# Two small loads moved behind the weights' loads, and one preparation moved ahead of the sums, in a four-stage transformer kernel

## The chip, the cores and the metric

The kernel runs on one core of one Trainium2 chip. Its time is the device time of one execution in microseconds (us). Before the change it was 930.57 us, the median of three runs (930.12 to 933.92). A core has a matrix engine (TensorE, PE in the profile), a vector engine (VectorE, DVE), an activation engine (ScalarE, ACT), a general engine (GpSimd, POOL) and a queue engine (SyncE, SP), which here issues nearly all loads and stores (the gathers and some of the last stores are GpSimd's). Each runs its own list of instructions in order, and semaphores between them say when data is ready.

## The reference

Four layers follow each other, each with a residual where there is one to add and a layer norm around it. Cut to what matters here:

```python
# x: (8, 512, 256)
qkv = x @ W_qkv                              # layer 0, retention with 16 heads of 16
ret = einsum('bhtd,bhsd->bhts', q, k) * decay
r   = einsum('bhts,bhsd->bhtd', ret, v) + einsum('bhtd,hde->bhte', q, past_kv) * 256
y   = groupnorm(r) * gn_weight[head] + gn_bias[head]
x   = layernorm(x + y)

def absmean(W):                              # layer 0, FFN with ternary weights
    gamma = mean(abs(W)) + 1e-6
    return sign(W / gamma) * minimum(round(abs(W / gamma)), 1)
h = layernorm(gelu(x @ absmean(W_fc).T)) * ln_w + ln_b
x = layernorm(x + h @ absmean(W_proj).T)     # W_fc (1024, 256), W_proj (256, 1024)

x = layernorm(x + linear_attention(x))       # layer 1, attention over heads per token
x = layernorm(x + mixture_of_experts(x))     # layer 1, 8 experts, top 2, capacity 160
```

A ternary weight needs the mean of the absolute values of the whole matrix before its first element can be made: the matrix must be loaded and summed, the sum spread over the 128 partitions, and only then can the elements be compared with half the mean.

## The kernel before

The work goes batch by batch (8 batches of 512 tokens, held as 4 chunks of 128 tokens). Each batch passes through the stages a1 (projection to q, k, v and retention), a2 (group norm, residual), b (FFN), bn, c1, c2 (layer 1's attention), and then the experts. Two preparations run once: `prepare_ffn` makes the ternary weights, and `prepare_l1` transposes layer 1's.

**The order of instructions is written by a planner.** The stages are generators; `interleave` picks the next one for TensorE by planned times. Work for the other engines is handed to `op(engine, cost, t, fn, ...)`, where t is the time from which it may start (its due time) and cost is the planner's duration. `op` looks for the first gap of the engine's planned time that is long enough, from t on, and the operations are issued in the order of the times so found. DVS means VectorE with a port that it shares with GpSimd: in the plan such operations, and GpSimd's, exclude each other. Loads (`dma`) take no time in the plan; those with one due time are issued in the order of the calls. The plan only sets the order of each engine's list. On the chip, an instruction starts when its engine is free and its semaphores are set.

**The start of the kernel.** SP issues, in this order: the identity matrix `ident`, x of batch 0, `wqkv`, the table of constants `cst`, `past` (the past state, 16 KB), the two vectors of the group norm into `gn` (weight and bias, 16 values each, given to all 128 partitions), W_fc in four pieces of 256 KB (tile `prepare`), W_proj in four pieces (tile `pr_w`), the two vectors `lnwb` of the FFN's layer norm, x of batch 1, and layer 1's small vectors.

VectorE's list at the start: three sums of W_fc (`threshold`, "fc_t"), `prepare_past`, the fourth sum, two kT operations (they scale the keys of batch 0 out of PSUM), `halves` (the threshold itself), 8 operations of `ternary` for W_fc, four sums of W_proj ("pr_t"), three masks of the first scores (scm), `halves` and 8 ternary operations for W_proj, masks and states, the prT products, and `prepare_gn`. `prepare_past` (L612, L617) writes `past_bd`, the past state as block-diagonal matrices, which TensorE reads from about 33 us on (L990). `prepare_gn` (L623, L624) writes `gnp`, read by the group norm of batch 0 at 64.9 us.

TensorE's list at the start: transposes of x (L348), 16 matmuls for q and k (L905), the sums of W_fc over the partitions (fc_ps, L650), v (L929), the first scores (L955), four matmuls that only fill a wait (L294), the sums of W_proj (pr_ps, L650), the transposes of the ternary W_fc (L713), further scores and retention (L990, L1003, L1012), and the transposes of the ternary W_proj (L726). GpSimd masks one of every four score tiles (scm) and makes padded queries (qz). ScalarE moves results out of PSUM. Line L205 is the planner's common line for all operations handed to `op` directly.

Of the kernel before, what the change touches and what calls it, by code (L numbers as in the profile page):

```python
# [20 lines left out]
P = 128  # L21
# [60 lines left out]
def tile_layers(ctx: ExitStack, tc: tile.TileContext, ins, out, at):  # L82
# [52 lines left out]
    ACT, DVE, POOL, SP, GELU, EXP, DVS, POOLD = range(8)  # L135
# [12 lines left out]
    class Plan:  # L148
        now = 0.0
        slow = 0.0  # L150
        t = 0.0
# [14 lines left out]
    def give(tag, t, n=1):  # L166
        Plan.free[tag] += [t] * n

    def take(tag, n=1):

        times = sorted(Plan.free[tag])
        assert len(times) >= n, tag
        Plan.free[tag] = times[n:]
        return times[n - 1]

    def op(engine, cost, t, fn, *args, use=None, drop=None, bank=None, **kw):


        if engine in (GELU, EXP):
            cost += 0.0 if engine == Plan.loaded else TABLE  # L180
            engine, Plan.loaded = ACT, engine
        users = [engine]
        if engine in (DVS, POOL):
            users.append("port")
        engine = users[0] = {DVS: DVE, POOLD: POOL}.get(engine, engine)
        t = t + HOP
        if use is not None:
            t = max(t, take(use) + HOP)
        if engine != SP:
            length = max(cost - OVERLAP[engine], 0.05)  # L190
            found = False
            while not found:
                found = True
                for user in users:
                    for a, b in Plan.busy[user]:
                        if t + length <= a:
                            break
                        if b > t:
                            t, found = b, False
            for user in users:  # L200
                bisect.insort(Plan.busy[user], (t, t + length))
                while Plan.busy[user][0][1] < Plan.t - 30.0:
                    Plan.busy[user].pop(0)
        Plan.count += 1
        heapq.heappush(Plan.events, (t, Plan.count, lambda: fn(*args, **kw)))  # L205
        t += cost
        if drop is not None:
            give(drop, t)
        if bank is not None:
            release(bank, t)  # L210
        return t
# [5 lines left out]
    def pe(cost):  # L217


        start = max(Plan.now, Plan.t)  # L220
        if start - Plan.now > 1.5:
            Plan.slow = start + (1.5 if start - Plan.now < 3.0 else 8.0)
        cost += min(max(Plan.slow - start, 0.0) / 2, cost)
        Plan.now = Plan.t = start + cost
        return Plan.now + PE_OUT

    def bank(name):
        i = Plan.banks.index(min(Plan.banks))
        assert Plan.banks[i] < HELD, name
        ps = psum.tile([P, 512], F32, tag=f"bank{i}", bufs=1, name=name)  # L230
        Plan.bank_of[id(ps)] = ps, i
        Plan.banks[i] = HELD
        return ps

    def release(ps, t):
        Plan.banks[Plan.bank_of.pop(id(ps))[1]] = t

    def need(t, n=1):

        while True:  # L240
            r = max(t + HOP_PE, sorted(Plan.banks)[n - 1] + HOP if n else 0.0)
            yield "pe", r if r < HELD else Plan.t + 0.5
            if not n or sorted(Plan.banks)[n - 1] <= Plan.t + 1e-6:
                return
# [324 lines left out]
    with ExitStack() as stages:  # L569
# [15 lines left out]
        def dma(t, out, in_):  # L585
            op(SP, 0.0, t, nc.sync.dma_start, out=out, in_=in_)
# [8 lines left out]
        past = ab.tile([P, 2, HD], F32, name="past")  # L595
        dma(0.0, past, ins["L0_attn_past_kv"].rearrange("(m h) d e -> (h d) m e", m=2))
        gn = ab.tile([P, 2, H], F32, name="gn")
        dma(0.0, gn[:, 0, :], ins["L0_attn_gn_weight"].partition_broadcast(P))
        dma(0.0, gn[:, 1, :], ins["L0_attn_gn_bias"].partition_broadcast(P))

        past_bd = ab.tile([P, 2, P], F32, name="past_bd")

# [20 lines left out]
                nc.vector.tensor_tensor(gnt, bc(gn[:, j, :], 1, 2), headsel, ALU.mult)  # L623
                nc.vector.tensor_reduce(gnp[:, j, :], gnt, AX.X, ALU.add)  # L624

        op(DVS, 1.0, 15.5, prepare_past)
        op(DVS, 0.85, 40.0, prepare_gn)


# [9 lines left out]
        def threshold(name, parts, ts):  # L639

            tot = fb.tile([P, len(parts)], F32, name=f"{name}_t")
            for i, (part, t) in enumerate(zip(parts, ts)):
                t = op(
                    DVE, 0.61, t, V.tensor_reduce, tot[:, i : i + 1], part, AX.X, ALU.add,
                    apply_absolute_value=True,
                )
            yield from need(t)
            ps = bank(f"{name}_ps")
            for i in range(len(parts)):
                T.matmul(  # L650
                    ps[:, 0:1], ones, tot[:, i : i + 1], start=(i == 0), stop=(i == len(parts) - 1)
                )
            half = fb.tile([P, 2], F32, name=f"{name}_h")

            def halves():
                nc.vector.tensor_scalar(
                    half[:, 1:2], ps[:, 0:1], 1.0 / (FF * D), 1e-6, ALU.mult, ALU.add
                )
                nc.vector.tensor_scalar(half[:, 0:1], half[:, 1:2], 0.5, None, ALU.mult)
                nc.vector.tensor_scalar(half[:, 1:2], half[:, 1:2], -0.5, None, ALU.mult)  # L660

            return half, op(DVE, 0.5, pe(0.5), halves, bank=ps)

        def ternary(qs, ws, half, t):

            ends = []
            for q, w in zip(qs, ws):
                e = op(DVS, 0.36, t, V.tensor_scalar, q, w, half[:, 1:2], None, ALU.is_lt)
                ends.append(op(
                    DVS, 0.64, e, V.scalar_tensor_tensor, q, w, half[:, 0:1], q, ALU.is_gt,  # L670
                    ALU.subtract,
                ))
            return ends

        def prepare_ffn():
# [12 lines left out]
            def half_row(x, i):  # L688
                return x[:, i // 2, i % 2 * 512 : (i % 2 + 1) * 512]
# [9 lines left out]
                        )  # L699

            op(SP, 0.0, 0.0, vectors)
            parts = [[big[:, k, i * 512 : (i + 1) * 512] for i in fours] for k in range(2)]
            half, t = yield from threshold("fc", parts[0], [12.0, 13.5, 14.7, 16.0])
            ready = ternary(parts[1], parts[0], half, t)
            parts = [[half_row(w, i) for i in fours] for w in (w_pr, q_pr)]
            half, t = yield from threshold("pr", parts[0], [17.0, 18.0, 19.0, 20.0])
            ready_pr = max(ternary(parts[1], parts[0], half, t))
            for n4 in range(NF // 4):
                for k in range(NK):
# [11 lines left out]
            for n2 in range(NF // 2):  # L721
                yield from need(ready_pr)
                ps = bank("pr_tp")
                for n in range(2):
# [5 lines left out]
                t = op(  # L730
                    ACT, 0.6, pe(0.46), A.copy,
                    raw[:, n2 * 2 : n2 * 2 + 2, :].rearrange("p n d -> p (n d)"), ps, bank=ps,
                )
# [17 lines left out]
            for f in range(NF):  # L751
                T.matmul(acc[:, :D], ones, prT[:, f, :D], start=(f == 0), stop=(f == NF - 1))
            mean = wk.tile([P, D], F32, tag="ex", bufs=EX, name="pr_mean_s")
            t = op(
                ACT, 0.4, pe(3.5), A.activation, mean, acc[:, :D], AF.Copy, scale=1.0 / FF,
                use="ex", bank=acc,
            )
# [5 lines left out]
            t = e  # L763
# [989 lines left out]
        def after(*keys):  # L1753
# [3 lines left out]
        half = B // G  # L1757
# [10 lines left out]
            ],  # L1768
            [
                (("p", 0), [], {"b8": 2}, prepare_ffn()),  # L1770
                (("p", 1), [], {"m4": 1}, prepare_l1()),
            ],
# [89 lines left out]
```

## Time and profile before

| | before |
|---|---|
| runs, median (lowest to highest) | 930.57 us (930.12 to 933.92) |
| the profiled execution's own time | 931.42 us |
| its span in the profile | 929.6 us |
| mean granted TensorE clock | 0.982 |
| bytes moved by DMA | 60.69 MB |

The span goes from the first to the last instruction; 1.8 us of the profiled execution lie around it. In the profile a line such as `15.92 0.45 DVE L612 ... past_bd<-cst,past` says when an instruction began, how long it took, its engine and line, and which tile it writes from which. Instructions of one kind that follow each other are put together (x3), and the first start and the stretch from the first start to the last end are given. In brackets stands how long the engine had been idle, and what ended the wait. A table of stretches gives, for each, the busy time of the engines, the granted clock of TensorE as a share of full speed, and the mean busy share of the 16 DMA engines. The DMA queue's waits say what SP waited for before it could issue.

### The profile page before, as it was taken

The page shows a single profiled execution, that of the slowest core. Times are in us where ns is not written, and L with a number is a line of the kernel's source. Part 1 is how long each engine was busy: PE and PEld are TensorE (multiplying, and loading weights), DVE is VectorE, ACT ScalarE, POOL GpSimd, SP SyncE. Part 2 cuts the span into 40 slices and gives each one's busy share as a digit, 9 for nine tenths or more (in the row PEclk, how much of TensorE's full clock was granted, in tenths as well). Part 3 has the DMA queues.
Part 4 walks back from the last instruction along what each step waited for, and adds up shares of the span by engine and source line. Part 5 has one row for each costly group of instructions (what it writes and reads, how often), then busy time and mean ns, then how long its engine had stood idle before and what let it go on. Part 6 is the DMA issues. An engine that isn't in the chain of part 4 may idle for free. (4 is left out here: it accounts for less than half of the span.)

```text
span 929.6 us, 18769 instructions
## 1 busy us (share of the span) xinstructions
PE 881.7 (95%) x7628; PEld 687.9 (74%) x7628; DVE 607.9 (65%) x1530; ACT 453.0 (49%) x866; POOL 397.2 (43%) x404
## 2 busy tenths in 40 slices
PE   7899999999999999999999999999999999999892
PEld 4777777777767677677767676786787889999781
DVE  3945367669777847877887778578678654621223
ACT  2327356537652684486287535838536343122223
POOL 2425542744453263445434542732653332362233
PEclk9999999999999999999999999999999999999795
DMA  7030000001000100010020001050143356168742
GB/s 212 12 114 1 1 2 1 2 24 46 2 1 24 47 2 2 23 47 1 1 69 2 1 2 46 2 182 1 46 126 115 108 185 196 24 191 290 241 116 105
DMA packets 49894, 60.69 MB, mean 65 GB/s; under 512 B 5680, under 2 KB 44784, under 8 KB 49808
## 3 DMA queue, kind: packets, MB, share of 16 engines
q1 hardware_dynamic: 45952, 53.92, 17.4%
q0 software_dynamic: 3856, 5.57, 3.1%
q8 instruction: 60, 0.98, 0.4%
q14 instruction: 26, 0.21, 0.1%
HBM read 43.76 MB, written 15.73 MB: 64 GB/s over the span
## 5 line engine op out<-in xcount | busy, mean ns | idle before, releaser
L1167 PE MATMUL pr_ps<-prT,fT 128*128 128x257 f32 x512 | 117.4, 381 | 0.2 <-DVE f_ss L205 0.2
L1167 PEld LDWEIGHTS pr_ps<-prT,fT 128*128 128x128 f32 x512 | 95.2, 190 | 14.7 <-DVE f_ss L205 0.5
L205 POOL TENSOR_TENSOR fsq<-fsq,fsf 128x512 f32<-128x512 f32 x56 | 72.2, 1288 | 37.5 <-ACT fsf L205 35.3
L1530 PE MATMUL wi_ps<-xsT,wi 128*128 128x160 f32 x512 | 78.2, 308 | 0.1
L1559 PE MATMUL wo_ps<-e_hT,wo 128*128 128x160 f32 x512 | 74.5, 301 | 0.0
L1530 PEld LDWEIGHTS wi_ps<-xsT,wi 128*128 128x128 f32 x512 | 73.3, 196 | 1.3 <-ACT xsT L205 0.6
L205 DVE TENSOR_TENSOR hm<-hs,cst 128x512 f32<-128x512 f32 x96 | 60.2, 675 | 19.6 <-PE hs L1306 19.1
L1559 PEld LDWEIGHTS wo_ps<-e_hT,wo 128*128 128x128 f32 x512 | 70.8, 190 | 1.8 <-issue 1.5
L205 DVE TENSOR_TENSOR scm<-sc,cst 128x512 f32<-128x512 f32 x96 | 60.8, 679 | 15.4 <-PE sc L955 15.4
L205 ACT ACTIVATE e_hT<-wi_ps 128x480 f32<-128x480 f32 (+1 forms) x48 | 25.3, 526 | 87.4 <-PE wi_ps L1530 87.4
L205 POOL TENSOR_TENSOR ln_rs<-ln_rs,mhalf 128x4 f32<-128x4 f32 x32 | 33.3, 1040 | 80.7 <-DVE ln_rs L205 80.7
L205 POOL DMA_INDIRECT y_d<-eo,srci x21 | 32.8, 1561 | 71.4 <-ACT eo L205 35.7
L205 POOL TENSOR_TENSOR scm<-scm,cst 128x512 f32<-128x512 f32 x32 | 41.2, 1289 | 49.7 <-ACT scm L205 49.7
L205 DVE STREAM_TRANSPOSE hT<-pad 128x512 f32<-128x512 f32 x64 | 59.3, 959 | 3.5 <-ACT pad L205 3.0
L905 PE MATMUL qk_ps<-xT,wqkv 128*128 128x512 f32 x128 | 60.6, 617 | 1.0 <-ACT xT L205 1.0
L1247 PE MATMUL qk_ps<-l1T,x2T 128*128 128x512 f32 x128 | 61.5, 603 | 0.0
L205 POOL TENSOR_TENSOR hm<-hm,cst 128x512 f32<-128x512 f32 x32 | 41.1, 1284 | 33.5 <-ACT hm L205 33.5
L1138 PE MATMUL fc_ps<-x1T_l,fcT 128*128 128x512 f32 x128 | 53.8, 420 | 0.6 <-DVE x1T_l L205 0.5
L205 POOL TENSOR_SCALAR pad<-pad,lamv 128x128 f32<-128x128 f32 x32 | 12.0, 374 | 97.9 <-DVE pad L205 97.9
L1138 PE MATMUL fc_ps<-x1T_h,fcT 128*128 128x512 f32 x128 | 50.2, 392 | 0.0
L205 ACT ACTIVATE x<-x,ln_nb,ln_rs 128x256 f32<-128x256 f32 x64 | 33.2, 589 | 33.7 <-DVE ln_nb L205 33.5
L205 DVE COPY eoT<-wo_ps 128x320 f32<-128x320 f32 x16 | 7.8, 488 | 62.4 <-PE wo_ps L1559 62.4
(257 smaller groups left out, 2015.9 us busy)
## 6 DMA issues: line engine op xcount, KB each, us to landing
wi<-in_L_ffn_wi SPq DMA_DIRECT2D x13, 1024.0 KB, 6.8
wo<-in_L_ffn_wo SPq DMA_DIRECT2D x13, 1024.0 KB, 7.9
x<-in_L_attn_x SPq DMA_DIRECT2D x8, 512.0 KB, 3.9
x_d<-a SPq DMA_DIRECT2D x8, 512.0 KB, 3.0
y_d<-a SPq DMA_DIRECT2D x8, 512.0 KB, 4.2
z<-y_d SPq DMA_DIRECT2D x8, 512.0 KB, 6.1
out<-z SPq DMA_DIRECT2D x8, 512.0 KB, 3.5
prepare<-in_L_ffn_W_fc SPq DMA_DIRECT2D x4, 256.0 KB, 9.2
```

Of the source, the lines that this page charges most:

```text
L205: heapq.heappush(Plan.events, (t, Plan.count, lambda: fn(*args, **kw)))
L905: T.matmul(ps, wqkv[:, k, which * D + m * P : which * D + (m + 1) * P], xT[:, k, :], start=(k == 0), stop=(k == NK - 1),)
L1138: T.matmul(ps, fcT[:, k, f * P : (f + 1) * P], x[:, k, :], start=(k == 0 and x is low), stop=(k == NK - 1 and x is high),)
L1167: T.matmul(acc[:, : D + 1], hT[:, f, c * P : (c + 1) * P], prT[:, f, :], start=(f == 0), stop=(f == NF - 1),)
L1247: T.matmul(qk, x2T[:, k, cs], l1T[:, k, 0:2, :].rearrange("p a d -> p (a d)"), start=(k == 0), stop=(k == NK - 1),)
L1530: T.matmul(ps[:, f * CAP : (f + 1) * CAP], wi[:, k, (f3 + f) * P : (f3 + f + 1) * P], x[:, k, es], start=(k == 0), stop=(k == NK - 1),)
L1559: T.matmul(ps[:, m * CAP : (m + 1) * CAP], wo[:, f, m * P : (m + 1) * P], hT[:, f, :], start=(f == 0), stop=(f == NF - 1),)
```

## The change

The two `gn` loads are issued after the vectors of the FFN's layer norm instead of before W_fc. The due time of `prepare_past` goes from 15.5 to 10.5. The due times of the sums of W_fc go from 12.0, 13.5, 14.7, 16.0 to 12.5, 13.5, 14.7, 16.2, and those of W_proj from 17.0, 18.0, 19.0, 20.0 to 18.5, 19.5, 20.5, 21.5. No operation is added or taken away.

```diff
         past = ab.tile([P, 2, HD], F32, name="past")
         dma(0.0, past, ins["L0_attn_past_kv"].rearrange("(m h) d e -> (h d) m e", m=2))
         gn = ab.tile([P, 2, H], F32, name="gn")
-        dma(0.0, gn[:, 0, :], ins["L0_attn_gn_weight"].partition_broadcast(P))
-        dma(0.0, gn[:, 1, :], ins["L0_attn_gn_bias"].partition_broadcast(P))
...
-        op(DVS, 1.0, 15.5, prepare_past)
+        op(DVS, 1.0, 10.5, prepare_past)
         op(DVS, 0.85, 40.0, prepare_gn)
...
             op(SP, 0.0, 0.0, vectors)
+            for j, k in enumerate(("L0_attn_gn_weight", "L0_attn_gn_bias")):
+                dma(0.0, gn[:, j, :], ins[k].partition_broadcast(P))
             parts = [[big[:, k, i * 512 : (i + 1) * 512] for i in fours] for k in range(2)]
-            half, t = yield from threshold("fc", parts[0], [12.0, 13.5, 14.7, 16.0])
+            half, t = yield from threshold("fc", parts[0], [12.5, 13.5, 14.7, 16.2])
             ready = ternary(parts[1], parts[0], half, t)
             parts = [[half_row(w, i) for i in fours] for w in (w_pr, q_pr)]
-            half, t = yield from threshold("pr", parts[0], [17.0, 18.0, 19.0, 20.0])
+            half, t = yield from threshold("pr", parts[0], [18.5, 19.5, 20.5, 21.5])
             ready_pr = max(ternary(parts[1], parts[0], half, t))
```

## The prediction, made before the changed kernel was run

> **What bounds the kernel now.** I read the page's busy shares first, then stretches of the start, then instructions in order of time, then the DMA queue's own waits.
>
> ```profile
> PE 881.7 (95%) x7628; PEld 687.9 (74%) x7628; DVE 607.9 (65%) x1530; ACT 453.0 (49%) x866; POOL 397.2 (43%) x404
> ```
>
> TensorE sets the time over the whole kernel, but the edit touches only the first 45 us, so that stretch decides. By stretches of 5 us (after bounds and length: PE, PEld, DVE, ACT, POOL busy, granted clock, DMA share, GB/s):
>
> ```profile
> 10.00:15.00 5.00, 5.00 (x11) 2.29 (x10) 1.08 (x2) 1.17 (x2) 1.89 (x2) 1.00 0.85 268
> 15.00:20.00 5.00, 4.68 (x21) 3.22 (x20) 4.80 (x13) 0.37 (x1) 2.17 (x4) 1.00 0.68 150
> 20.00:25.00 5.00, 4.25 (x31) 2.93 (x30) 4.86 (x8) 1.98 (x5) 1.30 (x2) 1.00 0.56 164
> 25.00:30.00 5.00, 3.18 (x20) 2.95 (x21) 4.93 (x11) 1.14 (x2) 0.86 (x1) 0.90 0.01 3
> 30.00:35.00 5.00, 5.00 (x63) 3.83 (x62) 4.86 (x8) 2.26 (x5) 1.48 (x2) 0.76 0.00 0
> 35.00:40.00 5.00, 4.91 (x41) 3.71 (x40) 4.96 (x10) 3.25 (x7) 2.01 (x3) 1.00 0.01 2
> ```
>
> VectorE idles before 14 us and is full from 15 to 40; TensorE has holes at 20 to 30 and a lowered clock after them. So here VectorE sets the pace. Its order, beside TensorE and GpSimd:
>
> ```profile
> 8.12 9.00 PE L905 MATMUL qk_ps<-xT,wqkv 128*128 128x512 f32 x16
> ...
> 13.92 2.08 DVE L205 TENSOR_REDUCE fc_t<-prepare 128x1 f32<-128x512 f32 x3 [13.07 <-DMA prepare<-in_L_ffn_W_fc]
> ...
> 15.92 0.45 DVE L612 SCALAR_TENSOR_TENSOR past_bd<-cst,past 128x128 f32<-128x128 f32 x1
> ...
> 16.95 0.72 PE L650 MATMUL fc_ps<-fc_t,cst 128*128 128x1 f32 x6
> ...
> 17.27 0.67 DVE L205 TENSOR_REDUCE fc_t<-prepare 128x1 f32<-128x512 f32 x1
> 17.86 1.27 DVE L205 TENSOR_TENSOR kT<-qk_ps,cst 128x512 f32<-128x512 f32 x2
> 18.00 0.38 PE L650 MATMUL fc_ps<-fc_t,cst 128*128 128x1 f32 x2 [0.32 <-DVE fc_t L205]
> ...
> 19.06 0.14 DVE L656 TENSOR_SCALAR fc_h<-fc_ps 128x1 f32<-128x1 f32 x1
> ...
> 19.61 0.49 DVE L205 TENSOR_SCALAR prepare<-prepare,fc_h 128x512 f32<-128x512 f32 x1
> ...
> 23.68 1.82 DVE L205 SCALAR_TENSOR_TENSOR prepare<-prepare,fc_h 128x512 f32<-128x512 f32 x1
> 23.70 1.27 POOL L205 TENSOR_TENSOR scm<-scm,cst 128x512 f32<-128x512 f32 x1 [6.43 <-ACT scm L205]
> ```
>
> Read here: `prepare_past` (L612, L617) stands between the third and fourth sum of W_fc; the first sum waited 13.07 us for W_fc; the last ternary operation took 1.82 us where its like take 0.75, because GpSimd's operation began at the same moment. TensorE then waits for the sums of W_proj, which stand behind that operation:
>
> ```profile
> 26.25 0.88 PE L650 MATMUL pr_ps<-pr_t,cst 128*128 128x1 f32 x4 [2.00 <-DVE pr_t L205]
> ```
>
> The DMA queue's own waits:
>
> ```profile
> SPq L205 <- DMA gn<-in_L_attn_gn_weight: 2.1, 1, 2.1
> SPq L205 <- DMA cst<-in_constants: 1.7, 1, 1.7
> SPq L205 <- DMA wqkv<-in_L_attn_W_qkv: 1.3, 1, 1.3
> ```
>
> These fit one rule: an issue waits for the transfer eight places before it (the fourth W_fc piece at 8.00 for `wqkv`, the first W_proj piece at 10.05 for `cst`, the third at 12.97 for the group norm's weight).
>
> **Part 1, the two `gn` loads move past ten issues on SP's queue.** From the issue at 3.17 to the next at 4.75 they took 1.58 us, so W_fc's pieces start 1.58 us sooner. By the rule of eight the fourth piece now waits for `ident` (landed at 2.6), that is for nothing, against 8.00; the W_proj pieces wait for x, `wqkv`, `cst`, `past` (landed at 6.1, 7.9, 10.0, 10.2), so they go out by about 10.6 against 13.8. The two loads were 256 packets of 64 B; the DMA share was only 0.64 at 8 to 9 us and 0.49 at 10 to 11. So W_fc lands between no earlier (13.9 to 16.0) and some 2 us earlier; I take 1.5. It matters little, see part 2. Behind `gn` now: x of batch 1 and L1's vectors. x landed at 21.8 and is transposed at 58.6, cover 37 us. `gn` itself goes out at about 15 to 18 and took 9.0 to 9.8 us to land, so by 28; `prepare_gn` runs at 43.8, or about 41.8 after. Cover 14 us; without it VectorE would stop at `prepare_gn`, and behind it the prT operations that TensorE's later projection needs. Cost 0. Nothing moves on POOL's queue.
>
> **Part 2, `prepare_past` runs in VectorE's idle time.** Its four instructions hold VectorE from 15.92 to 17.27, 1.35 us. It needs `cst` and `past` (10.0 and 10.2), so it runs at about 10.2 to 11.6, ahead of the first sum (13.9, or about 12.4). Queued behind it are the W_fc sums, slack at least 0.8 us. Then the fourth sum ends at 16.7 at the latest (landing 16.0 plus 0.69), the first kT by 17.4, and the second kT can't start before its matmuls end at 17.12. So what ends last becomes TensorE: its eight fc_ps matmuls start at 16.95 without the 0.32 us wait and end at about 18.04 (last start 17.79 at steps of 0.12, plus 0.25) instead of 18.38. `halves` starts at 18.09 instead of 19.06, ternary at 18.64 instead of 19.61: **0.97 us**, not 1.35, and hardly dependent on part 1.
>
> **Part 3, where the gain goes.** The eighth ternary operation starts at 22.71 instead of 23.68. GpSimd's scm follows TensorE, which gains only 0.33, so it starts at 23.37: the VectorE operation is already running and ends at 23.46. The collision costs VectorE nothing (the next operations, sums of W_proj, ran at 0.67 beside GpSimd's 0.92 us operation). The 1.82 becomes 0.75: **1.07 us more**. The sums start at 23.39 instead of 25.43, so TensorE's hole of 2.00 us shrinks to about 0.3. Total **2.04 us** for VectorE up to 30 us.
>
> [...] The next collision is scm at 33.5 with the ternary of W_proj: one operation took 1.50 for 0.48, the next 0.85 for 0.75, 1.12 lost in all. [...] The rows show GpSimd's two short operations doing the waiting (1.53 instead of 0.98), so I keep 1.12 in both kernels.
>
> [...] By the rows TensorE then meets VectorE: W_proj's transposes need all its ternary operations, which ended at 36.1 and now at about 34.1, so TensorE waits there instead. I take 2.0.
>
> **Part 4, due times in the plan.** By the planner's arithmetic `prepare_past` takes 10.55 to 11.47, the sums 12.55, 13.55, 14.75, 16.25, kT 16.78 and 17.80 (before 17.00 and 17.80), `halves` 18.40 as before. The ternary starts at 18.95 as before, and the sums of W_proj, due from 18.55 instead of 17.05, find no gap before its end at 22.83 in either. So every later order is the same, on all engines; cost 0. If it were not, the later order would be redrawn, which no row can price.
>
> **Sum.** The order being fixed, and loads issued by the same events, what follows 36 us moves up together: TensorE has 94 to 99% busy in every stretch from 40 to 850. The span is 929.6 - 2.0 = 927.6, plus 1.8 around it 929.4 for the profiled execution (931.42 before), which is 0.85 above the median of 930.57. Predicted: **928.5 us**, 0.22% less.
>
> **Rivals.**
> - *Only the first step arrives.* The port collision comes back, at 23 us or with more of W_proj's ternary: gain 0.9 to 1.0, 929.6. For it: GpSimd's start is tied to TensorE, which moves less than VectorE. Against: 0.66 us margin (23.37 against 22.71).
> [...]
> - *The change doesn't do what it says*, since the weights' landing or TensorE's matmuls until 17.12 hide it: 930.5. For it: TensorE is full at 30 to 40. Against: it stands there behind sums that VectorE delays.
> - *Slower: `past` late.* It now heads VectorE's queue, with W_fc's traffic directly behind it. If it lands at L, sums and kT follow back to back: L + 1.35 + 2.7 + 1.2. That passes 19.06 from L = 13.8 on, 0.5% slower from L = 18.5. Landing at 15 would give 931.8. Against: it landed at 10.2 with three W_fc pieces already issued behind it.
>
> **Chances.** Forecast 0.58, with its own range 927.0 to 930.0; first step only 0.14; TensorE profits too 0.12; no effect 0.07; slower 0.09. From no change this kernel's measurement can tell about 0.5%, here 4.65 us: under 925.9 only the second rival reaches, with a window fewer, 0.10; over 935.2 a very late `past`, 0.05, or three more half-clock windows in the other cases, 0.03, together 0.08; within, 0.82. The runs before span 3.8 us, so the range is 926.0 to 931.3.
>
> **What would show it.** Right: `past_bd` before the first fc_t at 10 to 12 us; `halves` at about 18.1; the last W_fc ternary at 0.75; sums of W_proj at about 23.4; the wait of pr_ps under 0.5 us; the prT operations after pr_mean at about 44.8 instead of 46.82; `gnp` at about 41.8 without a wait. Wrong: another order of instructions after 20 us, a first fc_t that waits for `past`, or a gain at 40 us that is gone at 850.

## The result, and the profile after

The changed kernel takes 927.92 us (median; 925.99 to 930.48), the kernel before, on the same chip, 930.74 us (929.18 to 933.92). The ratio is **0.9968, with an interval of 0.9958 to 0.9977**: 2.1 to 3.9 us less, about 0.3%. The forecast was 928.5 us. The profiled execution took 930.26 us (span 928.5 us, granted clock 0.982), 1.16 less than the one before and well above its own median; a part of the reason comes at the end of this section.

TensorE still sets the time over the whole kernel. The busy line of the page after:

```profile
PE 881.2 (95%) x7628; PEld 688.0 (74%) x7628; DVE 607.0 (65%) x1530; ACT 452.5 (49%) x866; POOL 396.0 (43%) x404
```

The start by stretches of 5 us, kernel after (same columns as in the table of before):

```profile
10.00:15.00 5.00, 5.00 (x12) 2.23 (x11) 3.49 (x8) 1.17 (x2) 2.75 (x3) 1.00 1.05 296
15.00:20.00 5.00, 5.00 (x26) 4.04 (x25) 3.71 (x10) 1.02 (x3) 1.17 (x3) 1.00 0.53 127
20.00:25.00 5.00, 4.13 (x33) 2.77 (x32) 4.93 (x9) 1.33 (x4) 1.73 (x2) 1.00 0.21 62
25.00:30.00 5.00, 5.00 (x73) 4.17 (x73) 4.83 (x10) 2.91 (x6) 1.25 (x1) 1.00 0.01 3
30.00:35.00 5.00, 3.34 (x24) 2.32 (x24) 4.93 (x9) 2.43 (x5) 1.53 (x3) 1.00 0.00 0
35.00:40.00 5.00, 5.00 (x35) 4.13 (x32) 5.00 (x10) 1.15 (x3) 3.41 (x5) 1.00 0.02 3
```

VectorE works 3.49 us between 10 and 15, where it had worked 1.08, and now has room between 15 and 20 (3.71 for 4.80). TensorE's hole has moved from 25 to 30 into 30 to 35: it runs through W_fc's transposes and then waits for the ternary W_proj, which VectorE is still making. The instructions of the start in order of time, kernel after:

```profile
9.61 0.29 DVE L610 SCALAR_TENSOR_TENSOR past_bd<-cst,past 128x128 f32<-128x128 f32 x1 [8.75 <-DMA past<-in_L_attn_past_kv]
...
10.54 2.46 DVE L205 TENSOR_REDUCE fc_t<-prepare 128x1 f32<-128x512 f32 x4
...
16.18 0.69 DVE L205 TENSOR_TENSOR kT<-qk_ps,cst 128x512 f32<-128x512 f32 x1 [1.02 <-PE qk_ps L905]
...
16.97 0.16 DVE L654 TENSOR_SCALAR fc_h<-fc_ps 128x1 f32<-128x1 f32 x1
...
21.62 0.75 DVE L205 SCALAR_TENSOR_TENSOR prepare<-prepare,fc_h 128x512 f32<-128x512 f32 x1
22.25 1.27 POOL L205 TENSOR_TENSOR scm<-scm,cst 128x512 f32<-128x512 f32 x1 [6.08 <-ACT scm L205]
22.29 2.46 DVE L205 TENSOR_REDUCE pr_t<-pr_w 128x1 f32<-128x512 f32 x4
23.11 0.89 PE L648 MATMUL pr_ps<-pr_t,cst 128*128 128x1 f32 x4 [0.31 <-DVE pr_t L205]
...
28.72 1.85 DVE L205 SCALAR_TENSOR_TENSOR pr_q<-pr_w,pr_h,pr_q 128x512 f32<-128x512 f32 x1
28.75 1.28 POOL L205 TENSOR_TENSOR scm<-scm,cst 128x512 f32<-128x512 f32 x1 [4.77 <-ACT scm L205]
...
40.92 0.18 DVE L621 TENSOR_TENSOR gnt<-gn,cst 128x32 f32<-128x32 f32 x1
```

`prepare_past` runs as soon as `past` is there, the four sums follow without a break, and the second kT waits for TensorE (1.02 us), so TensorE ends last before `halves`. The last ternary operation takes 0.75 us, with GpSimd's mask starting 0.63 us behind it. TensorE waits 0.31 us for the sums of W_proj, where it had waited 2.00.

Laid side by side, the two profiled executions differ so:

| | before | after | difference |
|---|---|---|---|
| end of the q and k matmuls | 17.11 | 16.15 | -0.96 |
| `halves` | 19.06 | 16.97 | -2.09 |
| first sum of W_proj behind the ternary W_fc | 25.43 | 22.29 | -3.14 |
| start of the means of W_proj's transposes (pr_mean) | 42.74 | 39.90 | -2.84 |
| `prepare_gn` | 43.76 | 40.92 | -2.84 |

Two sizes make it up: 2.09 at `halves` and 1.05 from the collision that is gone (the last ternary operation's 1.82 against 0.75), less 0.3 at the next collision. TensorE's later matmuls keep a lead of 2.85 us, until 549.8 us. One stretch from there, between the same bounds in both profiles, and the 16 matmuls that follow the wait in it, first the kernel before:

```profile
549.85:553.25 3.40, 1.83 (x19) 1.05 (x15) 1.89 (x3) 3.40 (x8) 0.38 (x1) 1.00 0.00 0
...
552.44 3.77 PE L1400 MATMUL w_ps<-l1T,t 128*128 128x256 f32 x16 [1.57 <-ACT t L205]
```

and the kernel after:

```profile
549.85:553.25 3.40, 3.40 (x9) 2.61 (x9) 0.45 (x2) 0.92 (x3) 1.72 (x2) 0.50 0.00 0
...
549.60 5.41 PE L1400 MATMUL w_ps<-l1T,t 128*128 128x256 f32 x16 [1.58 <-ACT t L205]
```

The granted clock, the third figure from the end, is 1.00 and 0.50: after the change, TensorE ran this stretch at half clock. Its 16 matmuls took 5.41 us instead of 3.77, and the lead fell from 2.85 to 1.20. The two further profiles of the changed kernel (below) have full clock there, and a profile of a variant has such a stretch at 290 us instead. So this one execution shows 1.6 us less gain than the start earned, and the medians are the better witness of the whole.

### The profile page after: what moved, and what is told of

Read it like the earlier page. It is cut to its first block, busy times and chain, and to the rows that moved or that the text cites. A ratio compares the mean times of both kernels' runs of the same rounds, so it can differ in the third digit from the quotient of the medians.

```text
span 928.5 us, 18771 instructions
## 1 busy us (share of the span) xinstructions
PE 881.2 (95%) x7628; PEld 688.0 (74%) x7628; DVE 607.0 (65%) x1530; ACT 452.5 (49%) x866; POOL 396.0 (43%) x404
## 3 DMA queue, kind: packets, MB, share of 16 engines
HBM read 43.76 MB, written 15.73 MB: 64 GB/s over the span
## 5 line engine op out<-in xcount | busy, mean ns | idle before, releaser
L205 ACT ACTIVATE e_hT<-wi_ps 128x480 f32<-128x480 f32 (+1 forms) x48 | 25.2, 525 | 87.2 <-PE wi_ps L1530 87.2
L205 POOL TENSOR_TENSOR hm<-hm,cst 128x512 f32<-128x512 f32 x32 | 41.0, 1282 | 33.5 <-ACT hm L205 33.5
L205 POOL TENSOR_SCALAR pad<-pad,lamv 128x128 f32<-128x128 f32 x32 | 11.9, 372 | 98.0 <-DVE pad L205 98.0
L205 ACT ACTIVATE x<-x,ln_nb,ln_rs 128x256 f32<-128x256 f32 x64 | 33.2, 589 | 33.7 <-DVE ln_nb L205 33.5
```

## The experiments

A ratio is always to the kernel before on the same chip, with its 95% interval. The kernels of one group ran on one chip: the first four, the next four, the last four. Times inside a kernel are from its one profiled execution. One caution applies to them. The program of before was profiled a second time (the due times alone, below), and its `halves` came at 18.47, not 19.06. In both profiles VectorE works without a break from the first sum of W_fc to `halves`, so the 0.59 lies there: the first sum began at 13.43 instead of 13.92, and `prepare_past` took less. TensorE's q and k matmuls ended earlier too, at 16.43 instead of 17.11. No edit explains either. In the changed kernel it is these matmuls that end last before `halves`, and their end differs between executions with their start (first transpose at 6.22 us before, 5.68 after) and with the time from which they run at the full pace (one matmul every 0.85 us until about 11.9 us before and 10.5 after, then one every 0.43). It doesn't follow the loads: it is 15.5 to 17.1 in the four profiles with the `gn` loads in their old place, 15.7 to 16.7 in nine with them moved. So distances within one profile are compared where that is possible.

**1. The change without the moved loads.**

```diff
-            for j, k in enumerate(("L0_attn_gn_weight", "L0_attn_gn_bias")):
-                dma(0.0, gn[:, j, :], ins[k].partition_broadcast(P))
```
(and both loads back in front of W_fc)

> The changed kernel with the two gn loads back in their old place, so only prepare_past and the due times are moved. Theory (the forecast's own steps): with prepare_past out of the way the fourth sum of W_fc ends by 16.7 at the latest, TensorE's fc_ps matmuls end last, halves starts near 18.1 instead of 19.06, the eighth ternary operation escapes GpSimd (0.75 instead of 1.82), and the sums of W_proj start about 2.0 us earlier: about 928.6 against 930.7. Rival (the weights' earlier landing does the work): the first sum still waits to 13.9, halves stays near 19.06, and the time stays within 0.5 us of 930.7.

Measured: 930.51 us, ratio 0.9987 [0.9977, 0.9998], so 0.2 to 2.1 us. In order of time:

```profile
14.63 2.77 DVE L205 TENSOR_REDUCE fc_t<-prepare 128x1 f32<-128x512 f32 x4 [2.05 <-DMA prepare<-in_L_ffn_W_fc]
...
17.31 1.28 DVE L205 TENSOR_TENSOR kT<-qk_ps,cst 128x512 f32<-128x512 f32 x2
...
18.51 0.15 DVE L656 TENSOR_SCALAR fc_h<-fc_ps 128x1 f32<-128x1 f32 x1
...
23.14 1.83 DVE L205 SCALAR_TENSOR_TENSOR prepare<-prepare,fc_h 128x512 f32<-128x512 f32 x1
23.16 1.26 POOL L205 TENSOR_TENSOR scm<-scm,cst 128x512 f32<-128x512 f32 x1 [7.57 <-ACT scm L205]
```

`prepare_past` has gone ahead, and `halves`, at 18.51, is no earlier than in the second profile of before (18.47). The pieces of W_fc arrive so late that the sums end at 17.40 and both kT follow them back to back. TensorE's q and k matmuls had ended at 15.56, so VectorE still ends last, and the full collision is there. What the ratio gives, about 1.2 us, isn't seen in this profile: the ternary W_proj is done at 34.44 (36.10 and 35.52 in the two of before), but TensorE ran at half clock (granted 0.50) from 26.27 to 33.10, for 6.83 us where it was 3.40 in the first profile of before, and pr_mean starts at 42.32 (42.74 and 42.16).

**2. The moved loads alone.**

```diff
-        dma(0.0, gn[:, 0, :], ins["L0_attn_gn_weight"].partition_broadcast(P))
-        dma(0.0, gn[:, 1, :], ins["L0_attn_gn_bias"].partition_broadcast(P))
...
             op(SP, 0.0, 0.0, vectors)
+            for j, k in enumerate(("L0_attn_gn_weight", "L0_attn_gn_bias")):
+                dma(0.0, gn[:, j, :], ins[k].partition_broadcast(P))
```

> The kernel before with only the two gn loads moved behind the vectors of the layer norm; prepare_past keeps its place between the third and fourth sum. Theory now: W_fc lands by about 10 to 12 us, so the sums and prepare_past are all done before 15 us, ahead of TensorE's last q and k matmul; then the place of prepare_past doesn't matter, and this run alone gives as much as the whole change, 2.0 to 2.8 us (about 928.2). The two parts are then alternatives, not a sum. Rival (the forecast's sizing of part 1, landing 1.5 us earlier at most, so first sum at 12.4): prepare_past still delays the fourth sum to about 15.8, which also lies before 17.1, so the same 2.0. Second rival (additive parts): about half of the change, 929.4.

Measured: 928.35 us, ratio 0.9964 [0.9952, 0.9977]: **the whole gain of the change**.

```profile
10.10 2.20 DVE L205 TENSOR_REDUCE fc_t<-prepare 128x1 f32<-128x512 f32 x3 [9.25 <-DMA prepare<-in_L_ffn_W_fc]
...
14.70 0.68 DVE L205 TENSOR_REDUCE fc_t<-prepare 128x1 f32<-128x512 f32 x1
...
16.18 0.69 DVE L205 TENSOR_TENSOR kT<-qk_ps,cst 128x512 f32<-128x512 f32 x1 [0.21 <-PE qk_ps L905]
16.97 0.16 DVE L654 TENSOR_SCALAR fc_h<-fc_ps 128x1 f32<-128x1 f32 x1
```

W_fc's first sum starts at 10.10 instead of 13.9 or 13.4. `prepare_past` still stands between third and fourth sum, but the fourth ends at 15.38, before the second kT's matmuls do (16.15). Between the second kT and `halves` nothing differs from the changed kernel.

**3. Only the due time of `prepare_past`.**

```diff
-        op(DVS, 1.0, 15.5, prepare_past)
+        op(DVS, 1.0, 10.5, prepare_past)
```

> The kernel before with only the due time of prepare_past moved from 15.5 to 10.5. The planner then finds a gap at 17.18 for the first sum of W_proj (due 17.05) between the two kT operations, ahead of halves; two filling matmuls of TensorE fall away, all else keeps its order. Theory: the first W_proj sum waits for its piece (landed at 16.55 before) and pushes the second kT and halves by about 0.5, but one sum fewer stands behind the ternary (0.6 gained back): within 0.3 us of the run with the due times, about 928.6. Rival (the due times of W_proj matter): halves near 18.6 or later, the eighth ternary meets GpSimd again, 929.7 or more.

Measured: 930.67 us, ratio 0.9988 [0.9978, 0.9997], as in experiment 1 but in another way. With the old due times the planner puts a sum of W_proj between the two kT:

```profile
16.70 0.68 DVE L205 TENSOR_TENSOR kT<-qk_ps,cst 128x512 f32<-128x512 f32 x1
17.30 0.67 DVE L205 TENSOR_REDUCE pr_t<-pr_w 128x1 f32<-128x512 f32 x1
17.89 0.68 DVE L205 TENSOR_TENSOR kT<-qk_ps,cst 128x512 f32<-128x512 f32 x1
18.49 0.15 DVE L656 TENSOR_SCALAR fc_h<-fc_ps 128x1 f32<-128x1 f32 x1
```

The gap that `prepare_past` left is filled with work that isn't urgent. That is what the later due times of W_proj's sums prevent.

**4. Only the due times of the sums.**

```diff
-            half, t = yield from threshold("fc", parts[0], [12.0, 13.5, 14.7, 16.0])
+            half, t = yield from threshold("fc", parts[0], [12.5, 13.5, 14.7, 16.2])
...
-            half, t = yield from threshold("pr", parts[0], [17.0, 18.0, 19.0, 20.0])
+            half, t = yield from threshold("pr", parts[0], [18.5, 19.5, 20.5, 21.5])
```

> The kernel before with only the due times of the sums changed. The order of instructions is the same as before on every engine, so both theories expect no difference: 930.7, an interval that holds 1.000. [...]

Measured: 931.28 us, ratio 0.9997 [0.9985, 1.0008]. Each engine's order of instructions is that of before, so the edit is worth nothing alone, and the run shows what two equal programs differ by. Its profile is the second one of before:

```profile
18.47 0.14 DVE L656 TENSOR_SCALAR fc_h<-fc_ps 128x1 f32<-128x1 f32 x1
...
23.10 1.82 DVE L205 SCALAR_TENSOR_TENSOR prepare<-prepare,fc_h 128x512 f32<-128x512 f32 x1
24.85 1.27 DVE L205 TENSOR_REDUCE pr_t<-pr_w 128x1 f32<-128x512 f32 x2
```

The collision is there again, at 1.82. So it isn't an accident of one execution. Against this profile the first profile of the changed kernel leads by 2.26 us at 36 us, not by 2.85.

**5. The changed kernel again**, without an edit, as the measure of the next three.

> The changed kernel again, as the base of this group. Expected 927.9, 2.8 us under the kernel before. [...]

Measured: 928.49 us, ratio 0.9963 [0.9949, 0.9977]. `halves` at 16.54, 0.83 behind the end of the q and k matmuls (0.82 in the first profile).

**6 and 7. A delay ahead of `halves`**, on the changed kernel: extra sums of W_fc whose result nobody reads, one of 256 columns in 6, two of 512 columns in 7.

```diff
         def halves():
+            if name == "fc":
+                for w in [256]:          # in 7: [512, 512]
+                    nc.vector.tensor_reduce(idle, parts[0][:, :w], AX.X, ALU.add, apply_absolute_value=True)
```

> The changed kernel with one useless sum over 256 columns (about 0.4 us) on VectorE between the second kT and halves. Theory (collision decided by order of start): the eighth ternary operation then starts near 22.0, still ahead of GpSimd's mask (22.25 in the profile after), so the sums of W_proj start about 0.4 us later and no more: 0.2 to 0.5 us slower than the changed kernel. Rival (VectorE isn't what TensorE waits for): no loss at 23 us.

> The same with two useless sums over 512 columns (about 1.2 us). Theory: a ternary operation now starts after GpSimd's mask and one of them takes about 1.5 to 1.8 us, so 1.2 us of work costs about 2.2 to 2.3 us where the sums of W_proj start (near 24.6 instead of 22.3), and nearly all of it at the end: about 2 us slower than the changed kernel. Rival (no collision, or TensorE has the slack): 1.2 us or less at the sums, and under 1 us at the end.

Measured, 6: 928.8 us, ratio 0.9960 [0.9946, 0.9975], no loss. The sum of 0.41 us ran from 16.48 to 16.89, in part while VectorE would have waited for TensorE anyway. From the end of the q and k matmuls `halves` came after 0.97 us instead of 0.83. The expected loss of some tenths isn't shown.

Measured, 7: 929.61 us, ratio 0.9980 [0.9972, 0.9988]: by the ratios 1.6 us slower than experiment 5, by the medians 1.1 (the two intervals overlap a little).

```profile
17.38 1.40 DVE L657 TENSOR_REDUCE fc_idle<-prepare 128x1 f32<-128x512 f32 x2
18.69 0.15 DVE L660 TENSOR_SCALAR fc_h<-fc_ps 128x1 f32<-128x1 f32 x1
...
22.84 1.57 POOL L205 TENSOR_TENSOR scm<-scm,cst 128x512 f32<-128x512 f32 x1 [6.08 <-ACT scm L205]
23.33 1.63 DVE L205 SCALAR_TENSOR_TENSOR prepare<-prepare,fc_h 128x512 f32<-128x512 f32 x1
24.88 0.67 DVE L205 TENSOR_REDUCE pr_t<-pr_w 128x1 f32<-128x512 f32 x1
```

The collision is back: the last ternary operation takes 1.63 us. From the end of the q and k matmuls to the first sum of W_proj it is 8.15 us, in experiment 5 it is 6.14 (21.85 less 15.71): 1.1 us of lateness at `halves` (1.96 for 0.83 behind those matmuls) cost 2.0 us. That is the forecast's second step, run backwards.

**8 and 11. The next collision taken away.** In the changed kernel GpSimd's mask at 28.75 meets a ternary operation of W_proj. Here VectorE does that one mask:

```diff
-        def masked(name, ps, mask, t):
+        def masked(name, ps, mask, t, alone=False):
...
-                if i == 0:
+                if i == 0 and not alone:
...
-                scm, done = masked(f"scm_{b}_{c}", sc, triu, t)
+                scm, done = masked(f"scm_{b}_{c}", sc, triu, t, alone=(b == 0 and c == 1))
```

> The changed kernel with the first mask of batch 0's second score set made by VectorE out of PSUM instead of by ScalarE and GpSimd; one VectorE operation more (0.68), one ScalarE and one GpSimd operation fewer, every other order the same. Theory: the ternary operation of W_proj that took 1.85 in the profile after takes 0.75, TensorE's wait of 1.48 us before the transposes of the ternary W_proj shrinks by about 1.1, and the matmuls of pr_mean start about 1 us earlier: about 1 us faster than the changed kernel, 926.9. Rival: the padded queries take the mask's place in the collision, or the added 0.68 us eats it: within 0.4 us of the changed kernel.

> The kernel with the first mask of batch 0's second score set on VectorE, a second time: 0.5 to 1.0 us faster than the changed kernel in this group if the collision it removes counts to the end; equal to it if not.

Measured: 927.92 us, ratio 0.9957 [0.9943, 0.9972], and in the last group 928.14 us, 0.9968 [0.9956, 0.9980]. In the first profile the eight ternary operations of W_proj end 5.39 us after the `halves` of W_proj instead of 6.81 (experiment 5). With the extra mask on VectorE, pr_mean starts 22.11 us behind `halves` of W_fc (22.10 in the second profile), in the changed kernel 22.93 and, below, 22.63: 0.5 to 0.8 us of the 1.4 are left by then. (In experiment 5 it is 23.98; there TensorE ran at half clock from 33.53 to 36.94.) Yet the changed kernel itself, run beside the second, has 928.12:

**12. The changed kernel a third time.**

> The changed kernel a third time, as the base of this group: 927.9 to 928.5. [...]

Measured: 928.12 us, ratio 0.9971 [0.9956, 0.9985]. So what is saved at 40 us doesn't show at the end. The second profile of the variant leads this one by 1.49 us at pr_mean, of which 0.97 is TensorE's earlier end of the q and k matmuls. The lead holds up to 290 us, where the variant has a half-clock stretch:

```profile
290.00:293.30 3.30, 3.30 (x10) 2.66 (x9) 0.67 (x2) 0.71 (x2) 1.73 (x2) 0.50 0.03 11
```

The changed kernel had 1.00 there. Whether such stretches take the gain back as a rule, or one profile happened to, these runs can't tell. No gain is shown.

**9. The place in the queue kept, the small packets gone.** Two loads of a single row each, in one packet, are put where the group norm's two loads had stood. Their data is overwritten by `prepare_gn`, so they are an addition to the changed kernel.

```diff
+        for j in range(2):
+            dma(0.0, gnt[0:1, j, :], ins["L0_attn_W_qkv"][j : j + 1, :H])
```

> The changed kernel with two more loads in the old place of the gn loads, each of one row of 16 values into one partition (one packet of 64 B instead of 128), two issues on SP's queue ahead of W_fc as in the kernel before. Theory (the 256 packets of 64 B leave the DMA queues half idle for about 3 us): W_fc still lands as in the changed kernel, first sum before 11.5, DMA share near 1.0 at 8 to 11 us, time that of the changed kernel (928.2). Rival (the issue slots and the wait for the transfer eight places back delay W_fc): the fourth piece waits for wqkv to 7.5, the first sum comes at 12 or later, and the time goes back towards 930.5.

Measured: 928.97 us, ratio 0.9970 [0.9960, 0.9981], as the changed kernel on that chip. Stretches of 1 us, the last two figures being the DMA engines' busy share and GB/s; first the kernel before:

```profile
8.00:9.00 1.00, 1.00 (x2) 0.50 (x2) 0.00 (x0) 0.59 (x1) 0.00 (x0) 1.00 0.64 158
9.00:10.00 1.00, 1.00 (x3) 0.38 (x2) 0.00 (x0) 0.00 (x0) 0.00 (x0) 1.00 0.45 132
10.00:11.00 1.00, 1.00 (x3) 0.48 (x2) 0.00 (x0) 0.00 (x0) 0.00 (x0) 1.00 0.49 152
```

the changed kernel:

```profile
8.00:9.00 1.00, 1.00 (x2) 0.38 (x2) 0.00 (x0) 0.24 (x1) 0.00 (x0) 1.00 1.05 336
9.00:10.00 1.00, 1.00 (x2) 0.34 (x1) 0.36 (x2) 0.00 (x0) 0.00 (x0) 1.00 1.10 379
10.00:11.00 1.00, 1.00 (x3) 0.49 (x2) 0.96 (x4) 0.00 (x0) 0.00 (x0) 1.00 1.11 355
```

and the one-row loads in the old place:

```profile
8.00:9.00 1.00, 1.00 (x2) 0.42 (x2) 0.00 (x0) 0.26 (x1) 0.00 (x0) 1.00 1.04 324
9.00:10.00 1.00, 1.00 (x2) 0.34 (x1) 0.33 (x2) 0.00 (x0) 0.00 (x0) 1.00 1.09 374
10.00:11.00 1.00, 1.00 (x3) 0.46 (x2) 0.96 (x4) 0.00 (x0) 0.00 (x0) 1.00 1.11 356
```

With one-row loads the first W_fc issue comes at 3.87, and the fourth piece does wait for `wqkv` and goes out at 7.5 (4.75 and 8.0 in the kernel before, 3.17 and 5.1 in the changed one). Still W_fc is summed from 10.57 on, as in the changed kernel (10.54). So neither the two issues nor the wait for an earlier transfer accounts for the delay in the kernel before. The two `gn` loads with their 256 packets of 64 B do: with them in front, the DMA engines are half empty for three microseconds, and 132 GB/s flow where 374 could. It holds in every profile: the first piece of W_fc landed at 13.4 to 14.6 us in the four with these loads in front, at 9.8 to 10.5 us in the ten others.

The number and size of the packets can't be all of it. `past` comes in 256 packets of 64 B as well, ahead of W_fc in every kernel, and in the changed kernel they moved between 7.5 and 9.0 us, where the share above is 1.05. What sets the `gn` loads apart is that each reads the same 64 bytes 128 times. Whether that is the reason no run shows: the loads tried here differ from them in both, in the number of packets and in reading one row once.

**10. Due times as the arrivals now are**, a try at a faster version.

```diff
-        op(DVS, 1.0, 10.5, prepare_past)
+        op(DVS, 1.0, 9.4, prepare_past)
...
-            half, t = yield from threshold("fc", parts[0], [12.5, 13.5, 14.7, 16.2])
+            half, t = yield from threshold("fc", parts[0], [10.5, 11.1, 11.7, 12.3])
```

> The changed kernel with due times as its own profile shows the arrivals: sums of W_fc at 10.5, 11.1, 11.7, 12.3 instead of 12.5 to 16.2, and prepare_past at 9.4. The planner then puts the sums over the partitions between the second and third pair of q and k matmuls, halves and the ternary before the second kT, and redraws what follows on all engines. Theory (VectorE sets the pace from 15 to 40 us and is held by TensorE's q and k matmuls at 16): halves at about 14 instead of 17, the chain up to pr_mean 1 to 2.5 us earlier, 926 to 927. Rival (a redrawn order gives it back elsewhere): 929 or more.

Measured: **953.57 us**, ratio 1.0231 [1.0210, 1.0253]. At the start it does what it was meant to: `halves` at 13.81 us and pr_mean at 36.80, 3.1 us ahead of the changed kernel. But the plan is redrawn from there on. The costliest groups tell where the time went; the changed kernel's matmuls that only fill waits:

```profile
L294 PE MATMUL spare<-cst,cst_ident 128*128 128x256 f32 x76 | 18.5, 384 | 0.0
```

and with the new due times:

```profile
L294 PE MATMUL spare<-cst,cst_ident 128*128 128x256 f32 x178 | 43.1, 392 | 0.0
```

That is 24.6 us more of filling on the engine that bounds the kernel; the profiled execution is 25.2 us longer. All of TensorE's busy time grew by 18.2 us (881.2 to 899.4), so some 7 us are more waiting. The planner puts fillers where its plan has waits; which of the moved operations opened them, and whether the fillers cost the time or only stand in such waits, isn't shown.

## Why the prediction was right

The median forecast was 928.5 us and 927.92 was measured; on the other two chips 928.49 and 928.12. The account of what happens from `halves` on was right. That the first step came out as well is in part luck: the forecast gave the gain to `prepare_past` and called the weights' landing unimportant, and it was the landing that brought it. With W_fc landing no earlier, the lower end of its own estimate, the same argument still gave about 928.5; experiment 1, where the first sum came 0.7 us later than before, measured 930.51. By its own steps:

- **Part 1, the moved loads: mis-sized and misjudged.** The forecast took 1.5 us of earlier W_fc, between 0 and 2, from the queue's issue times, and said "It matters little, see part 2". W_fc's first sum began 3.4 us earlier (10.54 for 13.92; 2.9 against the second profile of before), for experiment 9's reason, and this part alone carries the gain (experiment 2). The DMA shares of 0.64 and 0.49 that the forecast itself quoted were the sign: from 8 to 10 us eight transfers were in flight, five of them large, and the engines were half idle (0.64 and 0.45), so something other than bytes held this queue up. That the loads' new place costs nothing was right: they went out from 11.66 us, and `prepare_gn` ran at 40.92 without a wait.
- **Part 2, `prepare_past` in idle time: right in the changed kernel, wrong in the reason.** `halves` came 0.82 us behind the q and k matmuls instead of 1.95, 1.13 us gained for 0.97 forecast. But "hardly dependent on part 1" fell: the step rested on those matmuls ending at 17.12 and on the fourth sum ending by 16.7, both from the one profile of before. In experiment 1 they came at 15.56 and 17.40, so VectorE ended last, and the step gave 0.2 to 2.1 us, under half of the change by the middle of the interval. Where W_fc is early, the step isn't needed (experiment 2). The two parts don't add up: with the loads moved, nothing is left for `prepare_past` to gain that these runs could show. The other 0.96 of the 2.09 at `halves` is TensorE's own earlier end, and the second profile of before has 0.68 of it without any edit.
- **Part 3, the collision: right.** 1.07 forecast, 1.05 measured. It comes with late `halves` in the two profiles of before and in experiments 1, 3 and 7, and in the three profiles of the changed kernel and in experiments 2, 6, 8, 9 and 11 the operation takes 0.75. What plan and forecast call a port shows in the profile after only so: an operation of 0.75 us takes 1.85 beside GpSimd's mask of 1.28, while the four sums of W_proj keep their 0.68 each beside another of 1.27. In experiment 7 it is the later of the two that loses most: GpSimd's mask began at 22.84 and took 1.57 (1.27 in the profile after), the ternary operation began at 23.33, took 1.63, and ended 0.55 us after the mask. Alone it takes 0.75, so it did not wait quite to the end. In the profiles of before and of experiment 1 the ternary operation's record begins 0.01 to 0.02 us ahead of the mask's (23.68 and 23.70), and still it is the one that takes 1.82: so close together, the records don't tell which was first. "I keep 1.12 in both kernels" for the next collision was 0.29 too low for the profile after: three operations took 1.85, 0.70 and 0.84 us where they take 0.75, 0.48 and 0.75 alone, 1.41 lost. In the third profile of the changed kernel two took 1.50 and 0.85, and 1.12 was right.
- **The clock.** The forecast let TensorE wait for the ternary W_proj and took 2.0, and in the profile after that held: the half-clock stretch of before (granted 0.50 from 29.0 to 32.4 us) is gone, W_fc's transposes and the next scores are 0.95 and 0.66 us shorter, and TensorE then waits 1.48 us, up to 32.12, for the ternary W_proj. But the stretch isn't gone as a rule: in the second and third profile of the changed kernel one comes at 33.53 and at 25.41. Nor does it keep its place: one program shows its first such stretch at 550, at 33.5 and at 25.4 us in its three profiles. The chances also count on TensorE profiting too and on half-clock windows, one fewer or three more; no run shows these terms, and what the runs showed in their place is one stretch more at 550 us, which took 1.6 us of the lead in the profiled execution.
- **Part 4, the order: right.** Apart from the moved `prepare_past` and the two moved loads, each engine's list is the old one, and due times alone do nothing (experiment 4). "If it were not, the later order would be redrawn, which no row can price" has its price in experiment 10, for one such order: 25 us.
- **The sum** of 2.04 us compares with 2.1 to 3.9 by the ratio. At 36 us the three profiles of the changed kernel lead the two of before by 1.6 to 2.9 us (2.85, 2.23 and 2.66 against the first, about 0.6 less each against the second), so single profiles don't show the 2.04 to be too small. At 850 us the leads on the first are 1.17, 2.03 and 2.69: the sign of being wrong, "a gain at 40 us that is gone at 850", is seen in part in the one execution with the half-clock stretch at 550.

Of the rivals, "only the first step arrives" is what the kernel does when W_fc stays late (experiments 1 and 3), and late `past` did not happen: it landed by 9.6 us.

## What to carry to other kernels

A small load given to all partitions is cheap in bytes and can be dear in place: 16 KB in front of 2 MB cost the transfers behind it some 3 us here, so such vectors go behind what is needed first. When a change has two parts that shorten the same wait, each must be measured alone, since one may be the whole of it. And where a planner fills waits with work, a due time is not a small edit: correct arrivals gave a start that was 3 us better and a kernel that was 25 us slower.

## What the runs showed of the hardware that was not expected

- 256 packets of 64 B ahead of 2 MB in large transfers: DMA busy share 0.45 to 0.64 from 8 to 11 us (0.16 to 0.40 in the second profile of before), against 1.05 to 1.11 with those packets elsewhere. They read the same 64 bytes 128 times; the 256 packets of 64 B of `past`, which don't, ran at a share of 1.05.
- A collision made lateness cost more than itself: in experiment 7, where the last ternary operation began 0.49 us behind the mask and took 1.63, 1.1 us at `halves` became 2.0 us at the next sums; in experiment 6, where it took 0.75, 0.14 us stayed 0.13.
- Half-clock stretches of 3.4 us also come in the full middle of the kernel: at 549.8 us in the profiles of the changed kernel and of experiments 2 and 9, at 551.9 in experiment 3, at 289.9 in experiment 11, and in the other profiles not there. In the 3.41 us before the one of the changed kernel TensorE was busy for 1.83. One cost 1.6 us, half of what this change gains. What decides whether one comes isn't shown.
